# Two-layer adjacency network on one core: an end in written order with seven x1 buffers, k and v of two batches first, and row means of batch 0 by TensorE

## The chip, the cores and the metric

The kernel runs on one core of a Trainium2 chip. The metric is the device time of that core in microseconds (us), the median of several runs. TensorE is the matrix engine and writes to PSUM; VectorE and ScalarE work on rows and read PSUM; GpSimd does small odd work and issues some DMAs; SyncE issues most DMAs. All numbers are float32.

## The reference

The input is x of 16 batches, each N = 1024 nodes by C = 256 channels, and one adjacency matrix adj (1024 x 1024) for all batches.

Layer 0, for each batch:

```
c = mean of x over the channels                       (one number a node)
A[n,m] = 2 | |sigmoid(c[m] - c[n]) - 0.5| - 0.5 |     = 1 - tanh(|c[m] - c[n]| / 2)
g = relu( (x^T (adj * A)) * para )                    -> queries q, 4 heads of 64
k, v = x @ kv_w
x1 = layernorm( x + softmax(q k^T * scale) v )
```

Layer 1:

```
A_hat = normalised (adj + I)
h = relu( batchnorm( (A_hat x1) W1^T + b1 ) )
o = batchnorm( h W2^T + b2 )
out = layernorm( x1 + o )
```

Both batch norms take their statistics over all 16 x 1024 rows, so each of them is a point at which every batch must be done.

## The kernel before

**Stages.** Layer 0 is attention, batch after batch; its result x1 goes to HBM. Then comes aggregation and the first linear map for each batch, with h going to HBM and its statistics kept; then h comes back for the second linear map, whose output o2T (channels on the partitions, 8 KB a partition and batch) stays in SBUF for all 16 batches; then the end: normalise o2T, turn it, add x1, layer norm, store.

**Written order.** In layer 0 the instructions of TensorE, ScalarE and VectorE stand in the order in which the Python code calls them (`tc.manual_schedule`). Each engine runs its own queue strictly in that order, so an instruction that waits holds up all that stands behind it on the engine. In the end stage of the kernel before no order is written, and a planner sets it. GpSimd and SyncE are not under the written order in either case.

**The pieces of a batch of layer 0** (`prologue`, from L643):
- `begin` (L653) sums x over the channels on VectorE (`csum`, L658), makes the column of means `ccol`, writes the negated means to HBM as 1024 single numbers (L663), and reads them back as a row on all partitions, `crow` (L665).
- `transpose_x` (L667, products in L672) turns x to `xT` by TensorE; VectorE copies it out of PSUM (L675). There are four of these pieces in a batch, each through a PSUM tile of the two-buffer pool `tile_t`.
- `weights_abs` and `weights_tanh` (L680, L685, ScalarE) make A from `crow` and `ccol`, one block of 128 nodes each; `weights_adj` (L689, VectorE) multiplies by adj. These stand in the list `side`.
- `values` (L731) and `keys` (L718) make v and k on TensorE, in PSUM tiles of `tile_t`; VectorE copies v (L735) and ScalarE copies k (L722). `graph_mm` (L701) makes g, with q in L707 and L710. These stand in `steps`: eight for v and k in turn, then sixteen of `graph_mm`.

**The main loop** runs over bursts of two units; a unit is 128 keys of one query half and one pair of heads. A burst has its scores (L775), the exp on ScalarE (L780), the outputs of the burst before (L796) and the sums of exp on VectorE (L803, L805). A batch has 16 bursts, u = 0 to 15. Between them, at `FULL = (0, 4, 6, 8, 10, 12)`, four steps of the next batch are placed, with pieces of `side` at the places in `SIDE`; the next batch's transposes come at u = 10 and 12. So while batch b's attention runs, batch b+1 is prepared. For batch 0 nothing runs that could hide the preparation: the kernel before makes its transposes, then its steps and sides in turn, then the transposes of batch 1 and six of batch 1's sides, and enters the loop.

**Loads at the start.** SyncE issues x of batch 0, adj (4 MB), kv_w, para, and then x of batch 1.

**The end before.** `load_x1` (L1147) fetches x1 into one of three buffers `xf` (pool `fin`). `residual2` (L1183) scales and shifts o2T on ScalarE (L1186), turns it by TensorE (L1197, PSUM from `tile_t`), adds it into xf on VectorE (L1202), and takes statistics there (L1204, L1205). `rsqrt` (L578, L580) is two small GpSimd operations; a last small VectorE one (L1209) makes the shift. `finish` (L1214) normalises in place in xf on ScalarE (L1217), and GpSimd issues the store (L1221). A buffer is free for the next x1 only when that store has read it.

Of the kernel before, what the change touches and what calls it, by code (L numbers as in the profile page):

```python
# [10 lines left out]
F32 = mybir.dt.float32  # L11
I32 = mybir.dt.int32
AF = mybir.ActivationFunctionType
ALU = mybir.AluOpType
# [4 lines left out]
P = 128  # L19
HALF = 512  # L20
EPS = 1e-5
# [494 lines left out]
def fast_path(  # L516
# [19 lines left out]
    nc = tc.nc  # L536
    B, N, C = x.shape
    H = 4
    D = C // H
    NCH = N // P  # L540
    CC = C // P
# [26 lines left out]
    ident = const.tile([P, P], F32, name="ident")  # L568
    make_identity(nc, ident)
    ones = const.tile([P, D], F32, name="ones")  # L570
    nc.gpsimd.memset(ones, 1.0)
    mhalf = const.tile([P, NCH], F32, name="mhalf")
    nc.gpsimd.memset(mhalf, -0.5)

    def rsqrt(dst, src, eps):
        n = dst.shape[1]
        if eps:
            nc.gpsimd.tensor_scalar(dst, src, eps, None, ALU.add)  # L578
            src = dst
        nc.gpsimd.tensor_tensor(dst, src, mhalf[:, :n], ALU.pow)  # L580
# [38 lines left out]
    with (  # L619
# [11 lines left out]

        def load_x(b):
            t = xp.tile([P, NCH, C], F32, tag="x", name=f"x_{b}")
            nc.sync.dma_start(t, x[b].rearrange("(n p) c -> p n c", p=P))
            st[b] = {"x": t}

        load_x(0)
        nc.sync.dma_start(adj_s, adj.rearrange("(n p) m -> p n m", p=P))
        nc.sync.dma_start(kvw_s, kv_w.rearrange("(c p) k -> p c k", p=P))
        nc.sync.dma_start(para_s, para.rearrange("o (c p) i j -> p (o c) (i j)", p=P))  # L640
        load_columns()

        def prologue(b):  # L643
# [7 lines left out]
                steps.append((f, a))  # L651

            def begin():  # L653
                s["xT"] = xTp.tile([P, CC, N], F32, tag="xT", name=f"xT_{b}")


                csum = small.tile([P, NCH], F32, tag="csum", name=f"csum_{b}")
                nc.vector.tensor_reduce(csum, xt, AX.X, ALU.add)  # L658
                s["ccol"] = small.tile([P, NCH], F32, tag="ccol", name=f"ccol_{b}")
                nc.vector.tensor_scalar(s["ccol"], csum, 1.0 / C, None, ALU.mult)  # L660
                ncol = small.tile([P, NCH], F32, tag="ncol", name=f"ncol_{b}")
                nc.vector.tensor_scalar(ncol, csum, -1.0 / C, None, ALU.mult)
                nc.sync.dma_start(c_d[b].rearrange("o (n p) -> p (o n)", p=P), ncol)  # L663
                s["crow"] = crp.tile([P, N], F32, tag="crow", name=f"crow_{b}")
                nc.sync.dma_start(s["crow"], c_d[b][0].partition_broadcast(P))  # L665

            def transpose_x(c, half):  # L667
                if c == 0 and half == 0:
                    begin()
                pt = tile_t(f"pxT_{b}_{c}_{half}")  # L670
                for j in range(4):
                    nc.tensor.transpose(  # L672
                        pt[:, j * P : (j + 1) * P], xt[:, 4 * half + j, c * P : (c + 1) * P], ident
                    )
                nc.vector.tensor_copy(s["xT"][:, c, half * HALF : (half + 1) * HALF], pt)  # L675


            def weights_abs(n):
# [57 lines left out]
                    s["v"][:, 2 * pair : 2 * pair + 2, :].rearrange("p n c -> p (n c)"), pt  # L736
                )

            for c in range(CC):
                for half in range(2):  # L740
                    first.append((transpose_x, (c, half)))
            for i in range(4):
                step(values, i)
                step(keys, i // 2, i % 2)
# [113 lines left out]
        def run(fs, k):  # L858
            for f, a in fs[:k]:
                f(*a)  # L860
            del fs[:k]
# [114 lines left out]
        FULL = (0, 4, 6, 8, 10, 12)  # L976
        SIDE = {13: 2, 14: 2, 15: 2, 1: 2, 2: 2, 3: 2}
        with tc.manual_schedule(engines={mybir.EngineType.PE, mybir.EngineType.Activation, mybir.EngineType.DVE}):
            load_x(1)
            first, steps, side = prologue(0)  # L980
            run(first, 4)
            while steps:
                run(side, 6)
                run(steps, 2)
            next_first, next_steps, next_side = prologue(1)
            run(next_first, 4)
            run(next_side, 6)
            full, quarter, late = {}, {}, {}

# [34 lines left out]
            for j in range(len(bursts)):  # L1024
                b, u = j // PERB, j % PERB
                for i in bursts[j]:
                    scores(i)
                run(quarter.get(j, []), 9)
                if u == 0:
                    steps, side = next_steps, next_side  # L1030
                    next_first, next_steps, next_side = [], [], []
                if j:
                    back(j - 1)
                run(late.get(j, []), 9)
                if u == 5 and b + 2 < B:
# [102 lines left out]
    with (  # L1138
# [5 lines left out]
        ]  # L1144
        xf = {}

        def load_x1(b):  # L1147
            xf[b] = fin.tile([P, NCH, C], F32, tag="xf", name=f"xf_{b}")
            nc.sync.dma_start(xf[b], x1_d[b])

        with tc.tile_pool(name="hl", bufs=2) as hl:
            sg1, sh1 = batchnorm_coeffs(bn1_st, cols["g1"], cols["be1"], HC, "bn1")
            for b in range(B):
# [22 lines left out]
                            o2T[b][:, c, half * HALF : (half + 1) * HALF],  # L1176
                        )
                if b >= B - 3:
                    load_x1(b - (B - 3))

        sg2, sh2 = batchnorm_coeffs(bn2_st, cols["g2"], cols["be2"], CC, "bn2")

        def residual2(b):  # L1183
            for c in range(CC):
                o = o2T[b][:, c, :]
                nc.scalar.activation(  # L1186
                    o, o, AF.Identity, bias=sh2[:, c : c + 1], scale=sg2[:, c : c + 1]
                )
            xt = xf[b]
            st = small.tile([P, NCH, 6], F32, tag="ln_st", name=f"st_l1_{b}")  # L1190
            mv = small.tile([P, NCH, 2], F32, tag="ln_mv", name=f"mv_l1_{b}")
            for pair in range(NCH // 2):
                pt = tile_t(f"pf_{b}_{pair}")
                for j in range(2):
                    n = 2 * pair + j
                    for c in range(CC):
                        nc.tensor.transpose(  # L1197
                            pt[:, j * C + c * P : j * C + (c + 1) * P],
                            o2T[b][:, c, n * P : (n + 1) * P], ident,
                        )  # L1200
                xs = xt[:, 2 * pair : 2 * pair + 2, :].rearrange("p n c -> p (n c)")
                nc.vector.tensor_add(xs, pt, xs)  # L1202
                for n in (2 * pair, 2 * pair + 1):
                    nc.vector.bn_stats(st[:, n, :], xt[:, n, :])  # L1204
                    nc.vector.bn_aggr(mv[:, n, :], st[:, n, :])  # L1205
            rstd = small.tile([P, NCH], F32, tag="ln_rs", name=f"rs_l1_{b}")
            rsqrt(rstd, mv[:, :, 1], EPS)
            nmr = small.tile([P, NCH], F32, tag="ln_nm", name=f"nm_l1_{b}")
            nc.vector.scalar_tensor_tensor(  # L1209
                nmr, mv[:, :, 0], -1.0, rstd, op0=ALU.mult, op1=ALU.mult  # L1210
            )
            return rstd, nmr

        def finish(b, rstd, nmr):  # L1214
            xt = xf.pop(b)
            for n in range(NCH):
                nc.scalar.activation(  # L1217
                    xt[:, n, :], xt[:, n, :], AF.Identity,
                    bias=nmr[:, n : n + 1], scale=rstd[:, n : n + 1],
                )  # L1220
            nc.gpsimd.dma_start(out[b].rearrange("(n p) c -> p n c", p=P), xt)  # L1221

        before = None
        for b in range(B):
            if b not in xf:
                load_x1(b)
            now = residual2(b)
            if before is not None:
                finish(b - 1, *before)
            before = now  # L1230
        finish(B - 1, *before)

# [40 lines left out]
```

## Time and profile before

| what | value |
|---|---|
| time, median of 3 runs | 2851.09 us (2850.2 to 2852.6) |
| span of the profiled execution | 2849.5 us |
| TensorE busy | 2665.9 us, 94% of the span |
| VectorE busy | 1429.2 us, 50% |
| ScalarE busy | 1153.8 us, 40% |
| GpSimd busy | 191.0 us, 7% |
| HBM read and written | 99.89 MB and 67.44 MB |
| first matrix product of a graph step (batch 0) | at 58.1 us |
| first scale and shift of the end (L1186) | at 2686.4 us |

The page of a profile has a table of busy times, then the span cut into 40 slices in which a digit is the busy share in tenths, then the groups of instructions. A line `ACT wg L680 <- DMA crow<-c` in a list of waits says that ScalarE stood idle before line 680's instruction until the DMA that writes crow from c had landed. An order of time has the start, the length, the engine, the line, out<-in, the shape and how many such instructions were merged.

### The profile page before, as it was taken

To read this page: it belongs to the slowest core of one execution; us is meant where nothing else is said; L and a number is where in the kernel's file an instruction comes from. 1 tells how busy PE (TensorE), PEld (TensorE's weight loads), DVE (VectorE), ACT (ScalarE), POOL (GpSimd) and SP (SyncE) were. 2 spreads that over 40 slices of the span, in tenths; PEclk is the share of its full clock that TensorE was granted. 3 is DMA by queue.
4 is the path that set the end of the run, shared out by engine and by line. 5 is a ranking of instruction groups with operands and counts; after the bars stand their busy time and mean duration, and the time that the engine had idled before them with its cause. 6 is when DMAs were issued, how large, how long until landed. Compare 5 with 4: busy or idle time off the path is not lost. (4 is left out here: it accounts for less than half of the span.)

```text
span 2849.5 us, 32440 instructions
## 1 busy us (share of the span) xinstructions
PE 2665.9 (94%) x13394; PEld 1160.2 (41%) x13394; DVE 1429.2 (50%) x2102; ACT 1153.8 (40%) x1349; POOL 191.0 (7%) x204
## 2 busy tenths in 40 slices
PE   5899999999999999999999998999999999999833
PEld 2344434434434434434434433444444444344432
DVE  2456666666666666666666676311111111333554
ACT  2444644645645645645645635111101100333473
POOL 0000000000000000000000002000000000000032
PEclk8999999999999999999999999999999999999855
DMA  4001011011011011011011011332112211244165
GB/s 133 8 8 31 9 38 31 9 38 31 9 38 31 9 38 31 9 38 31 9 38 31 21 33 31 111 133 89 59 76 87 85 49 59 106 160 148 73 222 194
DMA packets 123245, 169.51 MB, mean 59 GB/s; under 512 B 87760, under 2 KB 104656, under 8 KB 112848
## 3 DMA queue, kind: packets, MB, share of 16 engines
q1 hardware_dynamic: 113904, 100.22, 11.7%
q0 software_dynamic: 9184, 67.12, 5.9%
q8 instruction: 107, 1.75, 0.3%
q14 instruction: 50, 0.41, 0.0%
HBM read 99.89 MB, written 67.44 MB: 59 GB/s over the span
## 5 line engine op out<-in xcount | busy, mean ns | idle before, releaser
L780 ACT ACTIVATE p<-ps 128x1024 f32<-128x1024 f32 x512 | 495.5, 1020 | 148.1 <-PE ps L775 71.6
L775 PE MATMUL ps<-qT,kT 64*64 64x512 f32 x4096 | 495.1, 598 | 9.8 <-ACT p L780 9.8
L796 PE MATMUL po<-p,v 64*64 64x512 f32 x4096 | 486.4, 590 | 0.0
L805 DVE TENSOR_TENSOR acc<-acc,p 128x1024 f32<-128x1024 f32 x384 | 469.9, 1224 | 25.7 <-ACT p L780 3.2
L701 PE MATMUL pg<-wg,x 128*128 128x512 f32 x1024 | 451.4, 594 | 1.6 <-ACT kT L722 1.6
L962 PE MATMUL pagg<-ahT,x1l 128*128 128x512 f32 x1024 | 442.4, 592 | 0.0
L1092 ACT ACTIVATE hw<-ph,col_b 128x1024 f32<-128x1024 f32 x64 | 71.4, 1116 | 575.5 <-PE ph L1088 575.5
L962 PEld LDWEIGHTS pagg<-ahT,x1l 128*128 128x128 f32 x1024 | 194.2, 190 | 243.8 <-issue 243.6
L701 PEld LDWEIGHTS pg<-wg,x 128*128 128x128 f32 x1024 | 189.7, 190 | 231.9 <-issue 215.7
L796 PEld LDWEIGHTS po<-p,v 64*64 64x64 f32 x4096 | 158.7, 133 | 282.3 <-issue 281.9
L775 PEld LDWEIGHTS ps<-qT,kT 64*64 64x64 f32 x4096 | 144.8, 133 | 299.4 <-issue 223.7
L710 ACT ACTIVATE qT<-qT 128x512 f32<-128x512 f32 x64 | 40.4, 632 | 527.8 <-DVE qT L707 527.8
L1166 PE MATMUL po<-hl,w12T 128*128 128x512 f32 x512 | 222.5, 598 | 6.9 <-ACT hl L1157 6.9
L966 DVE TENSOR_TENSOR agg<-pagg,dinv_row 128x1024 f32<-128x1024 f32 x32 | 39.2, 1225 | 372.1 <-PE pagg L962 372.1
L1088 PE MATMUL ph<-agg,w12T 128*128 128x512 f32 x512 | 222.2, 592 | 0.0
L689 DVE SCALAR_TENSOR_TENSOR wg<-wg,adj_s 128x1024 f32<-128x1024 f32 x128 | 170.8, 1352 | 49.9 <-ACT wg L685 49.9
L851 POOL TENSOR_TENSOR x<-x,o 128x512 f32<-128x512 f32 x64 | 81.3, 1270 | 1413.0 <-DVE o L846 1412.9
L707 DVE SCALAR_TENSOR_TENSOR qT<-pg,para_s 128x512 f32<-128x512 f32 x64 | 44.1, 690 | 256.5 <-PE pg L701 256.5
L731 PE MATMUL pv<-kvw_s,xT 128*128 128x256 f32 x512 | 127.0, 393 | 35.4 <-DVE v L735 25.8
L1094 DVE BATCH_NORM_STATS2 bn_st<-hw 128x6 f32<-128x512 f32 x128 | 82.3, 685 | 150.9 <-ACT hw L1092 150.9
L680 ACT ACTIVATE wg<-crow,ccol 128x1024 f32<-128x1024 f32 x128 | 147.7, 1154 | 16.1 <-DMA crow<-c 16.1
L1166 PEld LDWEIGHTS po<-hl,w12T 128*128 128x128 f32 x512 | 98.1, 192 | 131.3 <-issue 121.8
(91 smaller groups left out, 1972.6 us busy)
## 6 DMA issues: line engine op xcount, KB each, us to landing
h<-hw POOLq DMA_DIRECT2D x16, 2048.0 KB, 6.6
hl<-h SPq DMA_DIRECT2D x16, 2048.0 KB
x<-in_x_dram SPq DMA_DIRECT2D x16, 1024.0 KB
x<-x POOLq DMA_DIRECT2D x16, 1024.0 KB, 4.2
x1l<-x SPq DMA_DIRECT2D x16, 1024.0 KB
xf<-x SPq DMA_DIRECT2D x16, 1024.0 KB
out_dram<-xf POOLq DMA_DIRECT2D x16, 1024.0 KB, 5.3
crow<-c SPq DMA_DIRECT2D x16, 512.0 KB
```

Source lines behind the costliest of these rows:

```text
L680: nc.scalar.activation(w, s["crow"], AF.Abs, bias=s["ccol"][:, n : n + 1])
L689: nc.vector.scalar_tensor_tensor(w, w, 1.0, adj_s[:, n, :], op0=ALU.subtract, op1=ALU.mult)
L701: nc.tensor.matmul(ps, xt[:, n, c * P : (c + 1) * P], s["wg", n][:, hs], start=(n == 0), stop=(n == NCH - 1),)
L731: nc.tensor.matmul(pt[:, j * C : (j + 1) * C], s["xT"][:, c, n * P : (n + 1) * P], kvw_s[:, c, C : 2 * C], start=(c == 0), stop=(c == CC - 1),
L775: nc.tensor.matmul(ps[kh * D : (kh + 1) * D, hd * HALF : (hd + 1) * HALF], kT[r, pr, ks], qT[r, pr, qh * HALF : (qh + 1) * HALF], start=Tr ...
L780: nc.scalar.activation(p, ps, AF.Exp)
L796: nc.tensor.matmul(g["po"][kh][hd * D : (hd + 1) * D, :], s["v"][r, m, h * D : (h + 1) * D], p[r, hd * HALF : (hd + 1) * HALF], start=(m = ...
L805: nc.vector.tensor_add(g["acc"], g["acc"], p)
L962: nc.tensor.matmul(ps[:, hs], x1l[b][:, m, c * P : (c + 1) * P], aht[m][:, hs], start=(m == 0), stop=(m == NCH - 1),)
L1088: nc.tensor.matmul(ps[:, hs], w1T[:, c, k * P : (k + 1) * P], t[:, c, hs], start=(c == 0), stop=(c == CC - 1),)
L1094: nc.vector.bn_stats(bn1_st[:, k, 2 * b + half, :], ht[:, k, half * HALF : (half + 1) * HALF])
L1166: nc.tensor.matmul(ps[:, hs], w2T[:, k, c * P : (c + 1) * P], ht[:, k, hs], start=(k == 0), stop=(k == HC - 1),)
```

## The change

Three things are rewritten.

1. **The end in written order.** The three engines' order is now set by the code. Four more x1 buffers (`fin2`) are taken where the buffers of h were, so seven loads can be out. `finish` writes its result into o2T, which is free by then, so an xf buffer waits no more for a store, and SyncE issues the store, then the load seven batches on. The scale and shift of the next batch stands ahead of the finish of the one before. The PSUM tiles alternate between `tile_o` and `tile_t`. The aggregation of the statistics leaves VectorE: ten small GpSimd operations join the two halves' means and variances and make the scale and the shift.
2. **k and v of two batches first.** Before the loop, k and v of batch 0, then the transposes and k and v of batch 1, then the graph products of batch 0 are made. The loop places no steps of batch 1 at u = 0 and 4, but eight sides. For this x of batch 0 is loaded in two parts and kv_w after it, adj comes in four parts, and x of batch 1 after the first of them.
3. **Row means of batch 0 by TensorE.** A matrix of -1/C times xT gives the negated means on all partitions in PSUM, in place of the trip through HBM. Batch 1 and all later ones keep that trip.

The diff, cut to its core:

```diff
+    ncmat = const.tile([P, P], F32, name="ncmat")
+    nc.gpsimd.memset(ncmat, -1.0 / C)
...
         def load_x(b):
             t = xp.tile([P, NCH, C], F32, tag="x", name=f"x_{b}")
-            nc.sync.dma_start(t, x[b].rearrange("(n p) c -> p n c", p=P))
+            src = x[b].rearrange("(n p) c -> p n c", p=P)
+            if b == 0:
+                for n in range(0, NCH, 4):
+                    nc.sync.dma_start(t[:, n : n + 4, :], src[:, n : n + 4, :])
+            else:
+                nc.sync.dma_start(t, src)
...
         load_x(0)
-        nc.sync.dma_start(adj_s, adj.rearrange("(n p) m -> p n m", p=P))
         nc.sync.dma_start(kvw_s, kv_w.rearrange("(c p) k -> p c k", p=P))
+        adj_src = adj.rearrange("(n p) m -> p n m", p=P)
+        for n in range(0, NCH, 2):
+            nc.sync.dma_start(adj_s[:, n : n + 2, :], adj_src[:, n : n + 2, :])
+            if n == 0:
+                load_x(1)
...
                 nc.vector.tensor_scalar(s["ccol"], csum, 1.0 / C, None, ALU.mult)
+                if b == 0:
+                    return
...
+            def row_of_means():
+                s["crow"] = tile_s("crow_0")
+                for half in range(2):
+                    hs = slice(half * HALF, (half + 1) * HALF)
+                    for c in range(CC):
+                        nc.tensor.matmul(
+                            s["crow"][:, hs], ncmat, s["xT"][:, c, hs],
+                            start=(c == 0), stop=(c == CC - 1),
+                        )
...
-            for c in range(CC):
-                for half in range(2):
-                    first.append((transpose_x, (c, half)))
+            for i in range(2 * CC):
+                first.append((transpose_x, (i // 2, i % 2) if b else (i % 2, i // 2)))
+            if b == 0:
+                first += [(begin, ()), (row_of_means, ())]
...
-            load_x(1)
             first, steps, side = prologue(0)
-            run(first, 4)
-            while steps:
-                run(side, 6)
-                run(steps, 2)
+            run(first, 6)
             next_first, next_steps, next_side = prologue(1)
+            for _ in range(8):
+                run(steps, 1)
+                run(side, 2)
             run(next_first, 4)
+            for _ in range(8):
+                run(next_steps, 1)
+                run(side, 1)
+            run(steps, 99)
             run(next_side, 6)
...
-                    for _ in range(4):
+                    for _ in range(4 if b or u > 4 else 0):
                         run(steps, 1)
                         if u <= 4:
                             run(side, 2)
+                    if not b and u <= 4:
+                        run(side, 8)
...
+            tc.tile_pool(name="fin2", bufs=4) as fin2,
+            tc.manual_schedule(
+                engines={mybir.EngineType.PE, mybir.EngineType.Activation, mybir.EngineType.DVE}
+            ),
+        ):
+            for b in range(3, 7):
+                load_x1(b, fin2)
...
-                pt = tile_t(f"pf_{b}_{pair}")
+                    pt = tile_t(f"pf_{b}_{pair}") if pair % 2 else tile_o(f"pf_{b}_{pair}")
...
-                    nc.vector.bn_aggr(mv[:, n, :], st[:, n, :])
-            rsqrt(rstd, mv[:, :, 1], EPS)
-            nc.vector.scalar_tensor_tensor(
-                nmr, mv[:, :, 0], -1.0, rstd, op0=ALU.mult, op1=ALU.mult
-            )
+                me, qe, mo, qo = (st[:, :, k] for k in (1, 2, 4, 5))
+                w = small.tile([P, 4, NCH], F32, tag="ln_w", name=f"w_l1_{b}")
+                rstd, nmr, dif, var = (w[:, k, :] for k in range(4))
+                pool = nc.gpsimd
+                pool.tensor_tensor(nmr, me, mo, ALU.add)
+                pool.tensor_tensor(dif, me, mo, ALU.subtract)
+                pool.tensor_tensor(var, qe, qo, ALU.add)
+                pool.tensor_scalar(var, var, 1.0 / C, EPS, ALU.mult, ALU.add)
+                pool.tensor_tensor(dif, dif, dif, ALU.mult)
+                pool.tensor_scalar(dif, dif, 0.25, None, ALU.mult)
+                pool.tensor_tensor(var, var, dif, ALU.add)
+                pool.tensor_tensor(rstd, var, mhalf, ALU.pow)
+                pool.tensor_tensor(nmr, nmr, rstd, ALU.mult)
+                pool.tensor_scalar(nmr, nmr, -0.5, None, ALU.mult)
...
-                    xt[:, n, :], xt[:, n, :], AF.Identity,
+                        y[:, n, :], xt[:, n, :], AF.Identity,
...
-            nc.gpsimd.dma_start(out[b].rearrange("(n p) c -> p n c", p=P), xt)
+                nc.sync.dma_start(out[b].rearrange("(n p) c -> p n c", p=P), y)
+                if b + 7 < B:
+                    load_x1(b + 7, fin if b < 3 else (fin2 if b < 7 else fin))
...
+            scale_shift(0)
+            coeffs = {}
+            for b in range(B):
+                coeffs[b] = residual2(b)
+                if b + 1 < B:
+                    scale_shift(b + 1)
+                if b:
+                    finish(b - 1, *coeffs.pop(b - 1))
+            finish(B - 1, *coeffs.pop(B - 1))
```

More of the change, by code (lines that the diff above doesn't have):

```diff
@@ L653, in begin @@
             def begin():
-                s["xT"] = xTp.tile([P, CC, N], F32, tag="xT", name=f"xT_{b}")
                 csum = small.tile([P, NCH], F32, tag="csum", name=f"csum_{b}")
@@ L667, in transpose_x @@
             def transpose_x(c, half):
+                if c == 0 and half == 0 and b:
+                    begin()
                 if c == 0 and half == 0:
-                    begin()
+                    s["xT"] = xTp.tile([P, CC, N], F32, tag="xT", name=f"xT_{b}")
                 pt = tile_t(f"pxT_{b}_{c}_{half}")
@@ L1145, in fast_path, with load_x1 @@
         xf = {}
-        def load_x1(b):
-            xf[b] = fin.tile([P, NCH, C], F32, tag="xf", name=f"xf_{b}")
+        def load_x1(b, pool):
+            xf[b] = pool.tile([P, NCH, C], F32, tag="xf", name=f"xf_{b}")
             nc.sync.dma_start(xf[b], x1_d[b])
@@ L1178, in fast_path @@
                 if b >= B - 3:
-                    load_x1(b - (B - 3))
+                    load_x1(b - (B - 3), fin)
         sg2, sh2 = batchnorm_coeffs(bn2_st, cols["g2"], cols["be2"], CC, "bn2")
[L1183 to L1187, printed above, removed]
-                )
[L1189 to L1192, printed above, removed]
-                pt = tile_t(f"pf_{b}_{pair}")
[L1194 to L1206, printed above, removed]
-            rsqrt(rstd, mv[:, :, 1], EPS)
-            nmr = small.tile([P, NCH], F32, tag="ln_nm", name=f"nm_l1_{b}")
-            nc.vector.scalar_tensor_tensor(
-                nmr, mv[:, :, 0], -1.0, rstd, op0=ALU.mult, op1=ALU.mult
-            )
-            return rstd, nmr
@@ L1214, in finish @@
[L1214 to L1217, printed above, removed]
-                    xt[:, n, :], xt[:, n, :], AF.Identity,
-                    bias=nmr[:, n : n + 1], scale=rstd[:, n : n + 1],
-                )
-            nc.gpsimd.dma_start(out[b].rearrange("(n p) c -> p n c", p=P), xt)
[L1223 to L1230, printed above, removed]
@@ L1231, in fast_path, with scale_shift, residual2, finish @@
-        finish(B - 1, *before)
+        with (
+            tc.tile_pool(name="fin2", bufs=4) as fin2,
[5 more added lines that the diff above has]
+                load_x1(b, fin2)
+            def scale_shift(b):
+                for c in range(CC):
+                    o = o2T[b][:, c, :]
+                    nc.scalar.activation(
+                        o, o, AF.Identity, bias=sh2[:, c : c + 1], scale=sg2[:, c : c + 1]
+                    )
+            def residual2(b):
+                xt = xf[b]
+                st = small.tile([P, NCH, 6], F32, tag="ln_st", name=f"st_l1_{b}")
+                for pair in range(NCH // 2):
+                    pt = tile_t(f"pf_{b}_{pair}") if pair % 2 else tile_o(f"pf_{b}_{pair}")
+                    for j in range(2):
+                        n = 2 * pair + j
+                        for c in range(CC):
+                            nc.tensor.transpose(
+                                pt[:, j * C + c * P : j * C + (c + 1) * P],
+                                o2T[b][:, c, n * P : (n + 1) * P], ident,
+                            )
+                    xs = xt[:, 2 * pair : 2 * pair + 2, :].rearrange("p n c -> p (n c)")
+                    nc.vector.tensor_add(xs, pt, xs)
+                    for n in (2 * pair, 2 * pair + 1):
+                        nc.vector.bn_stats(st[:, n, :], xt[:, n, :])
+                me, qe, mo, qo = (st[:, :, k] for k in (1, 2, 4, 5))
[12 more added lines that the diff above has]
+                pool.tensor_scalar(nmr, nmr, -0.5, None, ALU.mult)
+                return rstd, nmr
+            def finish(b, rstd, nmr):
+                xt = xf.pop(b)
+                y = o2T[b].rearrange("p c n -> p (c n)").rearrange("p (n c) -> p n c", c=C)
+                for n in range(NCH):
+                    nc.scalar.activation(
+                        y[:, n, :], xt[:, n, :], AF.Identity,
+                        bias=nmr[:, n : n + 1], scale=rstd[:, n : n + 1],
+                    )
+                nc.sync.dma_start(out[b].rearrange("(n p) c -> p n c", p=P), y)
[10 more added lines that the diff above has]
+            finish(B - 1, *coeffs.pop(B - 1))
```

## The prediction

> **What bounds the kernel now.** I read the page's slices first, then the busy time by stretch, then the waits of the first 170 us and of the last 165, and at the places these name the order of time of single engines.
>
> ```profile
> PE   5899999999999999999999998999999999999833
> PEclk8999999999999999999999999999999999999855
> ```
>
> TensorE is full from slice 3 to slice 37, so the time is TensorE's work there, and only the first two slices and the last three (71 us each) have room. In stretches (columns: length, then busy us and instructions of PE, weight loads, DVE, ACT, POOL, then clock, DMA share, GB/s):
>
> ```profile
> 0.00:58.10 58.10, 22.61 (x65) 14.62 (x65) 15.98 (x18) 19.76 (x21) 5.33 (x14) 0.85 0.59 163
> 58.10:85.60 27.50, 27.50 (x64) 12.21 (x65) 3.40 (x5) 1.89 (x3) 0.00 (x0) 1.00 0.00 1
> 85.60:143.50 57.90, 44.76 (x281) 19.50 (x279) 30.87 (x32) 33.51 (x37) 0.00 (x0) 0.88 0.05 10
> 2686.40:2849.50 163.10, 62.31 (x256) 49.21 (x256) 93.21 (x336) 100.93 (x160) 45.58 (x48) 0.51 0.55 187
> ```
>
> Up to 143.5 us TensorE is idle for 48.6 us (143.5 less 22.61, 27.50 and 44.76). From there on, code and order are those of the changed kernel too, so a shift of this point is a shift of the end. In the last 163 us no engine is full: ScalarE, the fullest, works for 100.93. What the start waits for (us in total, times, longest):
>
> ```profile
> ACT L680 <- DMA crow<-c: 38.1, 1, 38.1
> ACT wg L680 <- DMA crow<-c: 16.1, 1, 16.1
> PE pv L731 <- DVE v L735: 25.8, 3, 16.0
> ```
>
> The row of means, crow, goes to HBM and comes back, and ScalarE, which runs in written order, stands at the first weight until 38.1 us in batch 0 and for 16.1 us in batch 1. Behind it in the queues stand the copies of k (ScalarE) and of v (VectorE), and TensorE waits for their PSUM buffers: the third line. For the end, the waits of the queue that issues loads, and one of VectorE:
>
> ```profile
> SPq L1149 <- DMA out_dram<-xf: 152.0, 12, 54.0
> DVE xf L1202 <- DMA xf<-x: 24.1, 8, 4.0
> ```
>
> Every x1 load from the fourth waits for the store that frees one of three xf buffers. Beside a steady piece of ScalarE (two batches), these are the VectorE and GpSimd instructions whose time I use below:
>
> ```profile
> 2702.32 4.63 ACT L1186 ACTIVATE o<-o,bn_sh,bn_sg 128x1024 f32<-128x1024 f32 x4
> 2706.85 7.98 ACT L1217 ACTIVATE xf<-xf,nm_l,rs_l 128x256 f32<-128x256 f32 x16
> 2714.74 4.63 ACT L1186 ACTIVATE o<-o,bn_sh,bn_sg 128x1024 f32<-128x1024 f32 x4
> ```
> ```profile
> 2712.90 1.29 DVE L1202 TENSOR_TENSOR xf<-pf,xf 128x512 f32<-128x512 f32 x2 [2.28 <-DMA xf<-x]
> 2714.11 0.74 DVE L1204 BATCH_NORM_STATS2 st_l<-xf 128x6 f32<-128x256 f32 x2
> 2714.76 0.16 DVE L1205 BATCH_NORM_AGGREGATE mv_l<-st_l 128x2 f32<-128x6 f32 x1
> ```
> ```profile
> 2696.12 0.24 POOL L578 TENSOR_SCALAR rs_l<-mv_l 128x8 f32<-128x8 f32 x1 [10.36 <-DVE mv_l L1205]
> 2696.45 1.67 POOL L580 TENSOR_TENSOR rs_l<-rs_l,mhalf 128x8 f32<-128x8 f32 x1
> ```
>
> **What the Trainium skill says.** "ScalarE: Activation LUTs", section "What ACT_TABLE_LOAD costs": an ACTIVATE costs 186 ns plus 0.833 ns an element, 93 ns more for each pointer operand, and neighbours overlap by some 93 ns. The trace agrees: 128x256 with two pointers should take 585 ns and took 589, at a step of 493. "DMA: Bandwidth & Descriptors", section "Issuing engines are not separate DMA queues": DMAs from any engine run on the same 16 engines. So moving the output store from GpSimd's to SyncE's queue changes no bandwidth; the trace of before has no such store from SyncE. "TensorE: Matmul & The Clock Gate", Part 1: the array runs at half clock after some 3.4 us idle and wants as long of work to wake. The trace agrees: the first four k matmuls at 24.9 us took 2.62 us, those at 50.4 us 1.88.
>
> **The start, part by part.** Durations of TensorE at full clock, by steps in the same trace: a v or k step 1.75 us (four from 128.59 to 135.67 are 7.08), the 32 graph products of a batch 27.4 us, 16 transposes 2.0 (3.9 cold), scores and outputs of a burst 1.75 each.
> 1. Batch 0's row by TensorE: 4 products with ncmat, 8 instructions of 0.43, 3.4 us, added to TensorE's path. I take 4.5, since part is cold (bounds 3.4 and 5.2, twice the cold 2.62). It removes the HBM trip. x_0 lands at 6.66; its first half should land near 5.2, as half of its movement (1 MB at some 360 GB/s, 2.9 us) falls away. Transposes: 5.2 to 9.2. The row is ready at 13.7, after the 1.28 of table load the first weight starts at 15.1 instead of 39.4. VectorE's column sums (2.29) now follow its copies and end by 12.4, beside the row.
> 2. The new load order: kvw before adj, adj in four. The DMA view of the first 40 us has 300 to 420 GB/s there, so 0.5 MB of kvw (landed 21.3 before) comes by about 10, the first quarter of adj by 13, x_1 by 16 and the last quarter by 24. Each is ahead of its reader: nothing charged.
> 3. k and v of batch 0: 8 steps, 14 us, 13.7 to 27.7. ScalarE has 12 weight activations of 1.07 and 4 copies of 0.5 beside them, 15 us, ending near 30; it trails TensorE by little.
> 4. Batch 1's transposes: VectorE does csum_1 (2.29) first, so TensorE waits about 3 us; k and v of batch 1 run from 32.9 to 46.9. They come out of the bursts u = 0 and 4, where they were TensorE's 14 us.
> 5. Graph products of batch 0: 46.9 to 74.3 (before: 58.1 to 85.6). Batch 1's row still goes through HBM: begun at 28, it took 14.5 us in the trace (88.9 to 103.3), so it is there by 45, hidden under step 5. The 16.1 us wait goes.
> 6. Bursts 0 to 5: ScalarE sets the pace, because the weights of batch 1 are all there. From 75.7 on: 5 activations, then for each burst 1.85 of exp, and between them 5, 2, 1, 1 and 2 weight activations of 1.07, with a 0.6 copy of oT: the fifth burst's exps end at 104.6. TensorE's scores of burst 6 start at 103.7 (140.0 before), its first graph product at 107.3 instead of 143.56. Gain 36 us; I take 35, as VectorE's sums (23 of 28 us) can hold p buffers a little.
>
> **The end, part by part.** Seven xf buffers and y in o2T: loads wait only for ScalarE's reads, and four more are issued as hl comes free (from 2672), all some 10 us before their use. DMA per batch: a store and a load are 2.1 MB, at the 340 to 380 GB/s of the best slices of the DMA view 5.5 to 6.2 us, and only nine loads are left, so it stays under ScalarE.
> - ScalarE: from 2702.32 to 2714.74 are two batches, 6.21 each (2.27 scale and shift, 3.94 finish).
> - VectorE: 4 adds at a step of 0.605 and 8 statistics at 0.325 are 5.02 a batch. The aggregates, 8 times 0.08, and nmr go.
> - TensorE: 16 transposes in 3.9 us cold; with four PSUM tiles instead of two it runs ahead.
> - GpSimd: ten small operations instead of two, and no DMA. Three scalar ones 0.24, pow 1.67, gaps 0.085 (both in the lines above). A plain two-tensor one of 8 elements isn't in the trace: at least the 0.24 of the scalar one, at most the 0.65 of the 128x128 addition (L939). The pow instructions of 2, 4 and 8 columns (0.71, 1.04, 1.67) leave 0.39 at none, so I take 0.43. Sum: 6 x 0.43 + 0.72 + 1.67 + 0.77 = 5.7; ends 4.6 and 7.1. With handover 5.9.
>
> First finish: VectorE starts at 2689.75 as before, ends at 2694.8, GpSimd at 2700.8. Then 13 rounds of 6.21 to finish(13) at 2781.5. The chain of a batch, 1.1 for the transposes, 5.0 and 5.9, is 12.0 us, and ScalarE gives it two rounds, 12.4: hidden, barely. At the very end it shows: finish(15) starts 12.1 after finish(13), at 2793.6, and ends at 2797.6. From ScalarE's last instruction to the end took 8.8 (2840.69 to 2849.5), which I keep. End at 2806.4: 43 us less.
>
> Together 78 us: 2851.1 - 78 = 2773.
>
> **Rivals.** GpSimd becomes the bound of the end. For it: 5.7 is near 6.21, and the upper price of 7.1 is over it; then 15 rounds of 7.1 from 2702 end at 2821, a gain of 29, and the time is 2787. Against: pow's own offset. The start is worth less: if ScalarE's or VectorE's order holds TensorE through k and v as now, or half clock persists, half of step 6's gain stays, 20 us: 2788. Against it, crow's two waits are the only long ones there. Both better: GpSimd at 4.6 and the end's last store quicker from SyncE, with a warm start, 12 us more: 2761. The other side: 1 KB rows stored from SyncE's queue move slowly, and loads queue behind. At 100 GB/s 16 stores take 168 us and nine loads 22, so the end lasts 190 instead of 163, and with a lost start it is 2870. Against: x_0's 1 KB rows came at up to 389 GB/s.
>
> **How the numbers follow.** Forecast 0.57, GpSimd 0.2, weaker start 0.12, both better 0.08, slower 0.03. The range from 2759 to 2792 takes in all but the slow case and the outer parts of two. Faster 0.95, same 0.02, slower 0.03.
>
> **What would show it.** Right: first weight near 15 us; graph products of batch 0 near 47; no wait on crow in batch 1; in the end no load waiting for a store, ScalarE at 6.2 us a batch with no idle but before the first and last finish. Wrong: ScalarE waiting for GpSimd each batch, GpSimd's two-tensor operations over 0.5 us, VectorE waiting for xf loads, or TensorE idle over 25 us before its first graph product of batch 1.

## The result and the profile after

| kernel | median (lowest to highest) | runs | span of the profile |
|---|---|---|---|
| before | 2850.64 us (2849.06 to 2852.6) | 4 | 2849.5 us |
| changed | 2766.95 us (2765.6 to 2767.95) | 4 | 2763.3 us |

The ratio is 0.9706 with a 95% interval from 0.9689 to 0.9723: 83.7 us less, where 78 were forecast (2773, range 2759 to 2792). Between the two profiles there are 86.2 us. They lie in the two stages that were changed: batch 1's first graph product comes at 105.97 us instead of 143.56 (37.6), and the end, from its first scale and shift on, lasts 115.5 us instead of 163.1 (47.6). The remaining 1.0 us lies in between, where kernels with the same code there differ by as much (2541.8 to 2542.8 us in nine of the profiles below). The lines for these two points, each before and then after:

```profile
143.56 7.13 PE L701 MATMUL pg<-wg,x 128*128 128x512 f32 x16
```
```profile
105.97 7.13 PE L726 MATMUL pg<-wg,x 128*128 128x512 f32 x16
```
```profile
2686.38 11.45 ACT L1186 ACTIVATE o<-o,bn_sh,bn_sg 128x1024 f32<-128x1024 f32 x10 [20.30 <-DVE bn_sh L1131]
```
```profile
2647.79 6.91 ACT L1230 ACTIVATE o<-o,bn_sh,bn_sg 128x1024 f32<-128x1024 f32 x6 [20.01 <-DVE bn_sh L1163]
```

First the slices of the changed kernel, and its stretches: k and v of both batches, the graph products of batch 0, bursts 0 to 5, and the end (columns as before).

```profile
PE   9899999999999999999999999999999999999964
PEclk9999999999999999999999999999999999999975
```
```profile
0.00:44.90 44.90, 38.46 (x136) 25.83 (x137) 23.28 (x28) 21.61 (x24) 5.57 (x15) 0.96 0.63 211
44.90:72.50 27.60, 27.60 (x69) 11.99 (x67) 3.53 (x5) 2.47 (x4) 0.00 (x0) 1.00 0.00 1
72.50:106.00 33.50, 25.48 (x218) 7.97 (x217) 21.86 (x20) 29.93 (x32) 0.00 (x0) 0.95 0.00 1
2647.80:2763.30 115.50, 57.61 (x256) 47.29 (x256) 87.48 (x192) 99.59 (x160) 54.92 (x160) 0.62 0.74 251
```

TensorE's first slice has gone from 5 to 9, and its last three from 8, 3, 3 to 9, 6, 4. Up to 106 us TensorE stands idle for 14.5 us (6.4 and 8.0), not 48.6. In the end ScalarE has the same 100 us of work as before, in 115.5 us. In the waits of the first 140 us ScalarE has no line for crow any more; ScalarE's first wait is for VectorE's column of means, and TensorE's longest is for exps, in the bursts:

```profile
ACT L705 <- DVE ccol L670: 11.2, 1, 11.2
PE ps L801 <- ACT p L806: 8.0, 3, 5.8
```

In the end, SyncE's queue waits only for ScalarE to finish a batch that is then stored. No load waits for a store:

```profile
SPq L1275 <- ACT o L1271: 99.1, 16, 20.4
```

ScalarE in order of time, at the first finishes and at the last three:

```profile
2660.84 4.04 ACT L1271 ACTIVATE o<-xf,w_l 128x256 f32<-128x256 f32 x8 [6.14 <-POOL w_l L1264]
2664.78 2.36 ACT L1230 ACTIVATE o<-o,bn_sh,bn_sg 128x1024 f32<-128x1024 f32 x2
2667.05 4.03 ACT L1271 ACTIVATE o<-xf,w_l 128x256 f32<-128x256 f32 x8
...
2741.42 4.04 ACT L1271 ACTIVATE o<-xf,w_l 128x256 f32<-128x256 f32 x8
2746.17 4.04 ACT L1271 ACTIVATE o<-xf,w_l 128x256 f32<-128x256 f32 x8 [0.71 <-POOL w_l L1264]
2752.08 4.04 ACT L1271 ACTIVATE o<-xf,w_l 128x256 f32<-128x256 f32 x8 [1.87 <-POOL w_l L1264]
```

From the second finish to the fourteenth, 12 rounds take 74.37 us, 6.20 each, and ScalarE waits for nothing. Only the first finish and the last two wait for the coefficients. The coefficients of batch 0 on GpSimd, and a pair of batch 6 on VectorE:

```profile
2656.85 0.21 POOL L1255 TENSOR_TENSOR w_l<-st_l 128x8 f32<-128x8 f32 x1 [9.68 <-DVE st_l L1249]
2657.02 0.20 POOL L1256 TENSOR_TENSOR w_l<-st_l 128x8 f32<-128x8 f32 x1
...
2658.53 1.67 POOL L1262 TENSOR_TENSOR w_l<-w_l,mhalf 128x8 f32<-128x8 f32 x1
2660.28 0.20 POOL L1263 TENSOR_TENSOR w_l<-w_l 128x8 f32<-128x8 f32 x1
2660.57 0.24 POOL L1264 TENSOR_SCALAR w_l<-w_l 128x8 f32<-128x8 f32 x1
```
```profile
2694.45 0.67 DVE L1247 TENSOR_TENSOR xf<-pf,xf 128x512 f32<-128x512 f32 x1
2695.16 0.75 DVE L1249 BATCH_NORM_STATS2 st_l<-xf 128x6 f32<-128x256 f32 x2
2695.83 0.67 DVE L1247 TENSOR_TENSOR xf<-pf,xf 128x512 f32<-128x512 f32 x1
```

A plain two-tensor operation takes 0.20 us, so the ten last 3.96 us (2656.85 to 2660.81). On VectorE the step from an addition to its statistics is 0.71, and 0.67 from there to the next addition: 1.38 a pair, 5.52 a batch.

### The profile page after: what moved, and what is told of

Same layout as the page of the kernel before. It is cut to its first block, busy times and chain, and to the rows that moved or that the text cites. A ratio compares the mean times of both kernels' runs of the same rounds, so it can differ in the third digit from the quotient of the medians.

```text
span 2763.3 us, 32469 instructions
## 1 busy us (share of the span) xinstructions
PE 2657.1 (96%) x13402; PEld 1157.4 (42%) x13402; DVE 1423.9 (52%) x1957; ACT 1151.5 (42%) x1349; POOL 200.7 (7%) x317
## 4 chain that ended last, share of the span: by engine, by line
PE 74%; DVE 13%; ACT 7%; issue 4%; POOL 1%; DMA 0%; DVEq 0%; ACTq 0%; POOLq 0%
PE pagg L988 16%; PE pg L726 12%; PE ps L801 11%; PE po L822 10%; PE po L1198 8%; PE ph L1120 8%; DVE acc L831 5%; PE pk L743 3%; PE pv L756 2%; ACT p L806 2%; DVE x L593 1%; ACT o L1271 1%; DVE st_l L589 1%; ACT wg L705 1%; DVE acc L829 1%
## 5 line engine op out<-in xcount | busy, mean ns | idle before, releaser
L1120 PEld LDWEIGHTS ph<-agg,w12T 128*128 128x128 f32 x512 | 97.3, 190 | 122.5 <-issue 122.5
```

Of the source, the lines that this page charges most:

```text
L1120: nc.tensor.matmul(ps[:, hs], w1T[:, c, k * P : (k + 1) * P], t[:, c, hs], start=(c == 0), stop=(c == CC - 1),)
```

## The experiments

Each edit is to the changed kernel unless said otherwise. Times are medians; the kernel before, run beside them, took 2851.06, 2850.9, 2849.18 and 2848.6 us in the four sets. The changed kernel was not run again beside them: "more than changed" and "under changed" compare with its 2766.95 us from the first set, and up to 2.5 us of such a difference can be that of the sets. Where it matters, lengths within the profiles are given too.

### The end alone, and the start alone

The first kernel joins the code before the second layer's linear maps from before to the rest from changed; the second does the reverse.

> The end of the changed kernel behind the start of the kernel before. My theory: start and end are separate stages with a full TensorE between them, so their gains add. The profiles put 47.6 us of the gain into the end (163.1 us to 115.5), so about 2803 us (2800 to 2807), and an end of 115 to 116 us. Rival: part of the shorter end comes from what the new start leaves behind (order of loads, clock); then the end lasts over 120 us and the two halves don't add up to 84.

> The start of the changed kernel (row by TensorE, k and v of two batches first, loads in parts) before the end of the kernel before. My theory: 38 us less than before, about 2812 us (2809 to 2816). Rival: a start that runs earlier than the stages after it can use it is given back in the attention of batch 0 or 1; then under 30 us of it are left at the first scale and shift of the end.

Measured: 2803.15 us (ratio 0.983, interval 0.9814 to 0.9846) and 2812.74 us (0.9865, 0.9849 to 0.9882): 47.9 and 38.3 us less than before, 86.2 together, beside 83.7 for both in one kernel; the 2.5 us between lie inside the intervals. The end of the first lasts 114.95 us (its scale and shift begins at 2685.95, its span is 2800.9). In the second, the 38.9 us by which batch 1's first graph product is earlier (104.67) are there at the end's first scale and shift (2646.99 instead of 2686.38, 39.4). So the two parts are separate, and nothing is given back on the way.

### What of the end is order, and what is buffers

With three x1 buffers:

```diff
-            for b in range(3, 7):
-                load_x1(b, fin2)
...
-                if b + 7 < B:
-                    load_x1(b + 7, fin if b < 3 else (fin2 if b < 7 else fin))
+                if b + 3 < B:
+                    load_x1(b + 3, fin)
```

> The changed kernel with three x1 buffers instead of seven; the result still goes to o2T, so a load waits only for ScalarE. My theory: from the last finish of batch b on, store and load of 1 MB each (some 7.5 us together), 5.0 us of VectorE, 4.0 of GpSimd and 3.9 of the next finish make a loop of three batches: 20.5 / 3 = 6.8 us a batch instead of 6.2, so 8 us more than changed, about 2775 (2770 to 2781). Rival, that the number of buffers is the gain of the end: 20 to 40 us more.

Three buffers, and the finish in place in them:

```diff
-                        y[:, n, :], xt[:, n, :], AF.Identity,
+                        xt[:, n, :], xt[:, n, :], AF.Identity,
...
-                nc.sync.dma_start(out[b].rearrange("(n p) c -> p n c", p=P), y)
+                nc.sync.dma_start(out[b].rearrange("(n p) c -> p n c", p=P), xt)
```

> The changed kernel with three x1 buffers and the finish in place in them, as before: a load waits for the store of the buffer. Order, PSUM tiles and the GpSimd coefficients stay as changed. My theory: the loop is store 6, load 5.5, VectorE 5.0, GpSimd 4.0, finish 3.9 and part of a scale and shift, 25 to 27 us for three batches, 8.2 to 9 a batch: 26 to 36 us more than changed, about 2797 (2790 to 2803), so that written order and coefficients alone are worth only 12 to 20 of the end's 47.6. Rival, that the written order is most of the gain: under 15 us more than changed.

Measured: 2784.24 us (0.9766, 0.975 to 0.9783), 17.3 more than changed, and 2803.74 us (0.9832, 0.9815 to 0.9848), 36.8 more. The three-buffer kernel with y apart: every third finish waits (first line of each loop), and VectorE waits for the loads of xf:

```profile
2661.03 4.04 ACT L1268 ACTIVATE o<-xf,w_l 128x256 f32<-128x256 f32 x8 [6.15 <-POOL w_l L1261]
...
2682.64 4.04 ACT L1268 ACTIVATE o<-xf,w_l 128x256 f32<-128x256 f32 x8 [2.89 <-POOL w_l L1261]
...
2704.59 4.04 ACT L1268 ACTIVATE o<-xf,w_l 128x256 f32<-128x256 f32 x8 [3.14 <-POOL w_l L1261]
```
```profile
DVE xf L1244 <- DMA xf<-x: 24.2, 10, 5.0
```

The loop of three batches takes 21.6 to 22.0 us, 7.2 to 7.3 a batch, not the 6.8 expected: VectorE has 5.52 for 5.0, and from the end of finish(0), 2665.07, to VectorE's start on the new x1, 2672.98, are 7.9 us for store and load. That is 14 us in 13 rounds, and the last two finishes wait for 3.4 us each. The number of buffers is therefore worth more than I expected (2784 lies outside my 2770 to 2781), though not the 20 of the rival.

In place, finish(0) at 2663.27 to finish(15) at 2790.11 are 126.84 us for 15 rounds, 8.46 each, as expected. The 36.8 us in all are a little over my 36, but the end accounts for 36.0 of them. The loads now wait for stores, and the chain that ended last goes through both (start, length, what):

```profile
SPq L1181 <- DMA out_dram<-xf: 41.6, 10, 4.5
```
```profile
2667.34 4.47 DMA out_dram<-xf
2671.82 3.95 DMA xf<-x
2675.77 2.82 ACT xf L1267 x6
2680.16 7.31 DMA xf<-x
```

The last of these lines shows something that my theory didn't have. The load for batch 4 waits for the store of batch 1, which was issued at 2673.54 and should be done some 4.5 us later; but SyncE's queue has the store of batch 2 (issued at 2679.73) ahead of it, so it starts some 2.1 us late. The same happens to the loads for batches 8 and 12 (2.6 and 2.2 us), all three on this chain. I estimate some 7 us of the in-place kernel's end for it, from these three delays; no run took it out.

By the lengths of the end in the profiles (163.1, 151.5, 133.7 and 115.5 us), the 47.6 us split into 11.6 for written order, PSUM tiles, coefficients and the store's queue together, 17.8 for the result's own place (the estimated 7 us of SyncE's queue among them), and 18.2 for the four more buffers, counted in this order. Written order and PSUM tiles were not taken apart.

### The coefficients back on VectorE

```diff
-                me, qe, mo, qo = (st[:, :, k] for k in (1, 2, 4, 5))
...
+                for n in range(NCH):
+                    nc.vector.bn_aggr(mv[:, n, :], st[:, n, :])
+                rsqrt(rstd, mv[:, :, 1], EPS)
+                nc.gpsimd.tensor_tensor(nmr, mv[:, :, 0], rstd, ALU.mult)
+                nc.gpsimd.tensor_scalar(nmr, nmr, -1.0, None, ALU.mult)
```

> The changed kernel with the aggregation of the statistics back on VectorE (eight aggregates a batch) and four GpSimd operations instead of ten. My theory: ScalarE with 6.2 us a batch is the bound and VectorE with 5.0 + 0.7 stays under it, so no change, within 2 us of the changed kernel (2767). Rival, that freeing VectorE was a source of the gain: 8 to 12 us more.

Measured: 2764.85 us (0.9699, 0.9686 to 0.9712), 2.1 under changed, at the edge of the expected 2. Its end lasts 114.1 us, 1.4 less than the changed one: the first finish comes 12.3 us after the first scale and shift, 13.05 in the changed kernel. So freeing VectorE of the aggregates was no source of the gain, and cost a little.

### What of the start is the row, and what is the order

Batch 0's row through HBM again (`begin` doesn't return early, and `row_of_means` isn't called):

> The changed kernel with batch 0's row of means through HBM again; loads and order as changed. My theory: the row's writes of single numbers stand behind 8 MB of loads, it lands at 30 to 38 us, the first weight starts 18 to 25 us later than in the changed kernel, k's copies stand behind it, and TensorE saves only the 3.4 us of the row: 15 to 27 us more, about 2787. Rival, that with k and v of two batches first TensorE has other work and the row's trip is hidden: under 5 us more.

The order of before for k and v, with the row by TensorE:

```diff
             run(first, 6)
+            while steps:
+                run(side, 6)
+                run(steps, 2)
             next_first, next_steps, next_side = prologue(1)
-            for _ in range(8):
-                run(steps, 1)
-                run(side, 2)
             run(next_first, 4)
-            for _ in range(8):
-                run(next_steps, 1)
-                run(side, 1)
-            run(steps, 99)
             run(next_side, 6)
```

with the loop's lines for u = 0 and 4 as before.

> The changed kernel with the order of the kernel before for k and v: those of batch 1 in the bursts u = 0 and 4, batch 1's transposes behind batch 0's graph products. The row by TensorE and the loads stay as changed. My theory: graph products of batch 0 end near 57 us, the wait of some 16 us on batch 1's row comes back, and batch 1's first graph product comes 58 us later, near 115 instead of 106: 9 us more than changed, about 2776 (2771 to 2782). So the row is worth some 28 us of the start and the new order 9. Rival, that the new order is most of it: 20 us more or beyond.

Measured: 2790.29 us (0.9787, 0.9772 to 0.9802), 23.3 more than changed, and 2778.11 us (0.9743, 0.9729 to 0.9756), 11.2 more. With the row through HBM, ScalarE waits for it until 36.6 us, and TensorE stands behind a copy of k; with the old order, the wait on batch 1's row is back (two lines from the first kernel, one from the second):

```profile
ACT L703 <- DMA crow<-c: 36.6, 1, 36.6
```
```profile
40.66 3.78 PE L754 MATMUL pv<-kvw_s,xT 128*128 128x256 f32 x8 [21.19 <-ACT kT L745]
```
```profile
ACT wg L705 <- DMA crow<-c: 16.1, 1, 16.1
```

Both theories held in size: the row is the larger half of the start, but only with the new order does the wait for batch 1's own trip disappear. The loads in parts, with kv_w ahead of adj, stayed in both kernels, so their share was not measured by itself; in the traces TensorE's first transposes begin at 4.26 us instead of 6.78.

### A third order for k and v

```diff
             run(next_first, 4)
-            for _ in range(8):
-                run(next_steps, 1)
-                run(side, 1)
+            run(side, 99)
             run(steps, 99)
```

with the loop's lines for u = 0 and 4 as before, so that k and v of batch 1 are made there.

> A third order: batch 1's transposes early, as changed, so that its row comes back under batch 0's graph products, but k and v of batch 1 in the bursts u = 0 and 4, as before. In the changed kernel ScalarE sets the pace of the bursts 0 to 5, and TensorE idles there for 8 us of 33.5. My theory: 14 us of k and v fill that idle time, so batch 1's first graph product comes near 97 us instead of 106 and the time is 5 to 11 us under the changed kernel, about 2758. Rival, that k's copies on ScalarE, behind exps and weights, hold TensorE's PSUM tiles so long that nothing is gained or the time is longer: 2766 to 2775.

Measured: 2759.77 us (0.968, 0.9667 to 0.9693), 7.2 under changed (5.8 between the profiles). Batch 1's first graph product comes at 101.02 us, 5 earlier, not 9: k and v fill TensorE's wait behind burst 0, but exps still hold it once, after four of the steps:

```profile
75.01 2.01 PE L801 MATMUL ps<-qT,kT 64*64 64x512 f32 x16 [1.71 <-ACT p L806]
```

### Stores by GpSimd again

```diff
-                nc.sync.dma_start(out[b].rearrange("(n p) c -> p n c", p=P), y)
+                nc.gpsimd.dma_start(out[b].rearrange("(n p) c -> p n c", p=P), y)
```

> The changed kernel with its stores issued by GpSimd again instead of SyncE. My theory: the same 16 DMA engines move them, ScalarE stays the bound, and only the last store's issue shows, since from ScalarE's last instruction to the end took 8.8 us before and 7.2 us as changed: 1 to 2 us more than changed, about 2768.5. Rival, that stores in GpSimd's queue hold up the next batch's coefficients behind them: 10 us more or beyond.

Measured: 2771.18 us (0.9726, 0.9713 to 0.974), 4.2 more than changed, where I had expected 1 to 2. Its end lasts 120.1 us, 4.6 more. After ScalarE's last instruction (2757.05 and 4.04 long, span 2769.9) it takes 8.8 us, 1.6 more than changed: that part is as expected. The other 3.0 are the rival's mechanism, once: the first store stands in GpSimd's queue, waits for ScalarE, and holds batch 1's coefficients behind it:

```profile
2662.56 0.24 POOL L1264 TENSOR_SCALAR w_l<-w_l 128x8 f32<-128x8 f32 x1
2667.17 0.99 POOL L1275 DMA_DIRECT2D out_dram<-o  x1 [4.37 <-ACT o L1271]
2668.19 0.22 POOL L1255 TENSOR_TENSOR w_l<-st_l 128x8 f32<-128x8 f32 x1
```

Later the coefficients come well ahead, and the queue costs nothing.

### Part of the finish off ScalarE, and both together

```diff
+                for n, eng in ((6, nc.vector), (7, nc.gpsimd)):
+                    eng.tensor_scalar(
+                        y[:, n, :], xt[:, n, :], rstd[:, n : n + 1], nmr[:, n : n + 1],
+                        ALU.mult, ALU.add,
+                    )
-                for n in range(NCH):
+                for n in range(6):
```

> The changed kernel with two of the eight slices of each finish taken from ScalarE, one to VectorE and one to GpSimd. My theory: ScalarE is the bound of the end at 6.2 us a batch; with 5.2 of ScalarE, 5.4 of VectorE and 4.7 of GpSimd the pace is 5.4 to 5.6, and 13 to 15 rounds give 8 to 12 us less than changed, about 2757. Rival, that DMA (2.1 MB a batch) or the chain of a batch over three engines sets the pace: under 3 us less.

> Both of the last changes, k and v of batch 1 in the bursts and the split finish. They lie in different stages, so by my theory their effects add: if each does what was expected alone, about 18 us under the changed kernel, 2749.

Measured: 2762.22 us (0.9694, 0.9681 to 0.9708), 4.7 under changed where 8 to 12 were expected, and 2754.62 us (0.9671, 0.9658 to 0.9684), 12.3 under, about the sum of 7.2 and 4.7. ScalarE waits half a microsecond in every round of the split finish, and VectorE has no gap (two successive slices of L1271 are a round):

```profile
2674.07 3.06 ACT L1276 ACTIVATE o<-xf,w_l 128x256 f32<-128x256 f32 x6 [0.52 <-POOL w_l L1264]
```
```profile
2681.52 0.40 DVE L1271 TENSOR_SCALAR o<-xf,w_l 128x256 f32<-128x256 f32 x1
2681.83 0.68 DVE L1247 TENSOR_TENSOR xf<-pf,xf 128x512 f32<-128x512 f32 x1
2682.55 0.75 DVE L1249 BATCH_NORM_STATS2 st_l<-xf 128x6 f32<-128x256 f32 x2
...
2687.36 0.40 DVE L1271 TENSOR_SCALAR o<-xf,w_l 128x256 f32<-128x256 f32 x1
```

The round is 5.84 us, and VectorE is the new bound: my 5.02 for its additions and statistics was too low.

### Additions ahead of the statistics

To the kernel with both:

```diff
                     nc.vector.tensor_add(xs, pt, xs)
-                    for n in (2 * pair, 2 * pair + 1):
-                        nc.vector.bn_stats(st[:, n, :], xt[:, n, :])
+                    if pair:
+                        for n in (2 * pair - 2, 2 * pair - 1):
+                            nc.vector.bn_stats(st[:, n, :], xt[:, n, :])
+                for n in (NCH - 2, NCH - 1):
+                    nc.vector.bn_stats(st[:, n, :], xt[:, n, :])
```

> The kernel with k and v of batch 1 in the bursts and the split finish, and in each batch of the end VectorE's addition of a pair ahead of the statistics of the pair before. In the split finish VectorE was the bound: its batch took 5.84 us, of which 5.52 are four additions and eight statistics, 0.12 more a pair than the 0.605 and 2 x 0.325 that I had read from additions and statistics among their like. My theory: the 0.1 us more stands between an addition and the statistics that read it; with another instruction between, a batch takes 5.3 to 5.5, and 15 rounds give 5 to 8 us less than with both changes alone (2754.6), about 2748. Rival: it is the cost of changing between the two kinds of instruction; then nothing changes, or 2 us more.

Measured: 2748.02 us (0.9645, 0.9632 to 0.9659), the fastest of all, 18.9 us under the changed kernel and 6.6 under both together. Its end lasts 103.1 us, 7.8 less than with both (110.8).

```profile
2691.35 0.43 DVE L1270 TENSOR_SCALAR o<-xf,w_l 128x256 f32<-128x256 f32 x1
...
2693.51 0.71 DVE L1243 TENSOR_TENSOR xf<-pf,xf 128x512 f32<-128x512 f32 x1
2694.10 0.78 DVE L1246 BATCH_NORM_STATS2 st_l<-xf 128x6 f32<-128x256 f32 x2
...
2696.66 0.44 DVE L1270 TENSOR_SCALAR o<-xf,w_l 128x256 f32<-128x256 f32 x1
```

A round is 5.31 us, and from an addition to statistics of another pair it is 0.59 instead of 0.71. So the 0.12 goes with reading what was just written, not with the change of instruction. ScalarE has no wait between its finishes any more: its round, 5.32 us, and VectorE's are now equally long.

## Why the prediction was right

The forecast's mechanism held in both stages; its sizes were off in both directions by a few microseconds.

- **The start, steps 1 and 2.** The first half of x landed at 4.26 us (5.2 said), the row was complete near 11.5 (13.7), the first weight began at 12.54 (15.1). ScalarE's wait ended with VectorE's column of means, and its table load ran beside the row's last product, so the row itself no longer set the first weight. No later load held anything up.
- **TensorE's clock in the start.** The row took 3.60 us here and up to 4.86 in other kernels with the same start. "TensorE: Matmul & The Clock Gate", Part 1, puts the waking at some 3.4 us of work, which would fit; but the clock on record is 1.00 from 4 to 13 us in this kernel and in the in-place one with 4.86, so the cause stays open. In the trace of before the record shows the waking at another place: 0.50 from 43 to 46.8 us and 1.00 from 47, with TensorE at work again from 43.56 (at 24.9 us, the place that the prediction names, it has 1.00). In the changed kernel it shows half clock later, too. At batch 1's transposes TensorE waits for VectorE for 1.94 us, a shorter idle than the 3.4 that the prediction takes from that page; the clock is 0.50 from 28.5 to 31.5 us, and the first v step takes 2.63 us. In the kernel with the start alone the clock stays 1.00 there and the step takes 1.99. These two places spread batch 1's first graph product from 104.67 to 107.83 us.
- **Steps 3 to 5.** k and v of both batches ended at 44.9 (46.9), the graph products at 72.5 (74.3). Batch 1's row was hidden: its trip ended by 42 us, 31 ahead of its first reader.
- **Step 6.** The exps of burst 5 (u = 5) ended at 102.9 (104.6) and the graph product came at 105.97 (107.3). The early landing and quick row carry through; the gain was 37.6, where I took 35 of 36.
- **The end, ScalarE.** 6.20 us a batch (6.21), the bound throughout. Splitting its work moved the bound, which shows it.
- **The end, VectorE.** 5.52, not 5.02. I had taken the steps between two additions and between two statistics; the step between an addition and the statistics that read it isn't among those, and the last experiment shows that it costs 0.12 more. Under ScalarE's 6.20 it hid.
- **The end, GpSimd.** 3.96, not 5.7. A small two-tensor operation takes 0.20 us, less than the 0.24 that I had as the lowest bound. The errors of VectorE and GpSimd went opposite ways and in part made up for each other: the first finish came 13.05 us after the first scale and shift (14.4 said), and finish(15) 10.66 after finish(13) (12.1).
- **The last store.** 7.2 us after ScalarE, not 8.8; with the store from GpSimd's queue it is 8.8 again.

Together the end lasted 115.5 us where my steps make 120.0: 1.4 at the first finish, 1.5 more at the last (the chain of 12.1), 1.6 in the store. Of the rivals, GpSimd as the bound fell with 0.20 us an operation; slow 1 KB stores fell with the end's 251 GB/s on average and no wait on them (that rival's sum doesn't close either: an end of 190 us and no gain at the start make 2878, not 2870); the weaker start didn't come. Of "both better", GpSimd's price and the quicker last store came true.

## What to carry to other kernels

Where a buffer is filled by a load, changed in place and stored, the store is part of the load's loop: count store, load, and each engine's turn, and divide by the buffers; a separate place for the result took the store out of this loop and was worth up to 17.8 us here. Look also at the order of the queue that issues both, where a load can stand behind a later store. A small tensor that goes through HBM to become a row costs all that stands behind its reader in that engine's queue, so look there, not at its bytes. Before moving work off the fullest engine, sum the next one with the steps between dependent instructions: two slices moved gave 4.7 us, and 6.6 more came only after VectorE's additions and statistics were interleaved.

## What was unexpected of the hardware

GpSimd's two-tensor operations on 128x8 took 0.20 us at a step of 0.17 when independent, while pow on the same shape took 1.67. On VectorE, statistics of what the addition before them wrote started 0.71 us after it, statistics of another pair 0.59, with 0.67 to 0.71 us for the addition in both cases. The program ended 7.2 us after ScalarE's last instruction with the last store (1 MB in rows of 1 KB) from SyncE's queue, and 8.8 us after it from GpSimd's. TensorE's clock was 0.50 from 28.5 to 31.5 us, after a wait of only 1.94 us at batch 1's transposes.
